# Layer 0's position bias: one more fold by DMA before the last product, one quarter of the sums on VectorE, and the tables on ScalarE

## The chip, the cores and the metric

The kernel runs on one core of a Trainium2 chip. The core has a matrix engine (TensorE, PE in the profile), VectorE (DVE), ScalarE (ACT), GpSimd (POOL) and a queue engine for transfers (SyncE, SP). Sixteen DMA engines move data for all of them. The metric is the device time of one execution in microseconds, lower is better; three runs of the kernel before gave 3259.31, 3259.72 and 3261.21, median 3259.72.

## The reference, cut to what matters

Four layers follow one another on an image batch. The change is in layer 0, a deformable attention on 2 images of 512 channels and 32 x 32 pixels, with 8 groups per image and 64 keys per group. Each key has a position that is computed from the data. For every one of the 1024 queries and every one of the 64 keys of a group, a small three-layer network turns the two coordinate differences into one number, the bias that is added to the attention score:

```python
pos = grid_q[:, :, None, :] - grid_kv[:, None, :, :]
bias = jnp.sign(pos) * jnp.log1p(jnp.abs(pos))
bias = jax.nn.relu(bias @ cpb_w1 + cpb_b1)      # 2 -> 128
bias = jax.nn.relu(bias @ cpb_w2 + cpb_b2)      # 128 -> 128
bias = (bias @ cpb_w3 + cpb_b3).reshape(b, GROUPS, H * W, Hd * Wd)
sim = jnp.einsum('bhid,bhjd->bhij', qh, kh) + bias
attn = jax.nn.softmax(sim, axis=-1)
out = jnp.einsum('bhij,bhjd->bhid', attn, vh)
```

That is 16 groups x 64 keys x 1024 queries through a network of width 128. All is in fp32.

## The kernel before, in words

**Tiling.** The loop over `quads` in `layer0` runs over 16 groups `u`, 8 steps `o` and two halves `half`: 256 quads of four keys each. A quad takes two calls. `first_hidden` makes the first hidden layer of four keys, 128 hidden units by 1024 queries for each key, with one VectorE instruction a key (L680): it adds a row table `x` and a column table `y`, broadcast against each other, and clips at zero. `second_hidden` multiplies these by the 128 x 128 weight (L704). A matmul makes 32 outputs of one key, and four keys stand side by side in the four strips of 32 rows of one PSUM tile, so a quad leaves four PSUM tiles, one for each quarter `q` of the 128 hidden units, each of 128 rows (4 keys x 32 units) by 1024 queries. Three such PSUM tiles exist (`c_ps_h`).

**The last layer.** The weights are sorted and scaled beforehand (`sorted_weights`), so that the last layer is a sum with signs. All quarters but the first hold units whose weights have the same sign in the same row, so quarters can be added without multiplying. ScalarE evicts each quarter with bias and ReLU (L709), multiplies the first by a sign (L711), GpSimd issues a DMA that adds the first quarter into the second (L716, 512 KB, accumulating), GpSimd adds the third into the fourth (L720), and one quad later `join` adds the second into the fourth (L723). The sum `z` has 32 rows a key. After a second half, `join` folds two quads: an accumulating DMA adds odd rows to even rows in the first half's sum (L725), another one even rows to odd rows in the second half's (L726), and SP copies the latter's odd rows into the former (L727). Then one tile holds eight keys with 16 rows each, and `last_product` sums the rows with a small matrix of signs on PE (L742): for every four quads one group of four matmuls, written to PSUM as scores. It is issued one such group of quads later, by the list `held`. `attend` adds query-key products, takes the softmax and multiplies by the values.

**The tables.** For two steps `o` at a time, SP loads `got`, the signed logarithms of the coordinate differences, from DRAM (L620). GpSimd makes `x` of it (L622, into SBUF); VectorE makes `y` (L665, into a PSUM bank) at the beginning of each first half. Two buffers exist for each of `got` and `x`.

**Order of the work.** The order on PE, ScalarE, VectorE and GpSimd is that of the program text. In each pass of the loop stand `first_hidden` of the next quad, `second_hidden` of this quad, perhaps a product, and then one step of the side work: `attend` and the output projection (`after`), or the positions, queries, keys and values of the next groups (`front`). So on ScalarE the order in a pass is: what `first_hidden` of the next quad puts there, the evictions of this quad, the step. On VectorE: the additions of the next quad, the step. Four buffers of h1 hold two quads.

**Buffers of the quarters.** Tags h20, h21, h22 and h23 have 2, 3, 2 and 6 buffers of 128 x 1024; the fourth holds `z` until its product or its copy is done.

The lines that the text below uses are L620, L622 and L665 (`table`), L680 (`first_hidden`), L704 to L727 (`second_hidden` and `join`), L742 (`last_product`), L366 (`share`'s and `projection`'s addition from PSUM) and L792 (the softmax's exponential).

Of the kernel before, what the change touches and what calls it, by code (L numbers as in the profile page):

```python
# [18 lines left out]
P = 128  # L19
# [16 lines left out]
    ("index", 1), ("row", 1), ("sixes", 16),  # L36
# [12 lines left out]
N_FOLDED, N_SINGLE = 56, 60  # L49
# [7 lines left out]
class Net:  # L57
# [40 lines left out]
    def layer0(self):  # L98
# [3 lines left out]
        with ExitStack() as ctx:  # L102
            keep = self.pool(ctx, "l0")
            self.l0qkv = keep.tile([P, 3, CT, P], F32, tag="qkv", name="qkv")
# [8 lines left out]
            self.l0w2 = keep.tile([P, P], F32, tag="w2", name="w2")  # L113
# [17 lines left out]
            self.hid2 = self.pool(ctx, "c_hid2", 1)  # L131
# [14 lines left out]
            with self.tc.manual_schedule(engines=engines):  # L146
# [23 lines left out]
                pairs[0]["xT"] = self.fone.tile([P, NB, P], F32, tag="xnT", name="xnT00")  # L170
# [15 lines left out]
                held, self.join, self.first_z = [], None, None  # L186
                batch = []
                for i, (u, o, half) in enumerate(quads):
# [9 lines left out]
                    z = self.second_hidden(u, o, half, h1, i + 1 == len(quads))  # L198
                    if half == 0:
                        batch.append((o % 2, z))  # L200
                    elif o % 2 == 1:
                        held.append((u, o, batch))
                        batch = []
                        if len(held) == 2:
                            v, last, zs = held.pop(0)
                            self.last_product(v, last, zs, sims, ps_s)
                            if last == 7:
                                if v == 8:
                                    self.advance(after, lambda: False)
                                    att = [  # L210
                                        apool.tile([P, N], F32, tag=f"att{t}", name=f"att{v}_{t}") for t in range(CT)
                                    ]
                                self.advance(front, lambda: "v" in pairs[v // 2])
                                after.append(self.attend(v, pairs[v // 2], sims.pop(v), att, ps))
                                if v % 8 == 7:
                                    after.append(self.projection(ps, att, ow, v // 8))
# [5 lines left out]
                (_, _, (ready, first)), = held  # L222
                self.last_product(u, o, [ready], sims, ps_s)
                self.single_product(u, o, 0, first[1], sims)
# [34 lines left out]
    def sorted_weights(self, keep):  # L259
# [7 lines left out]
        self.places = keep.tile([P, P + N_FOLDED + N_SINGLE], F32, tag="places", name="places")  # L267
        nc.scalar.dma_start(self.places, self.io["places"])
        before = keep.tile([P, P], F32, tag="before", name="before")
# [3 lines left out]
        names = ("pos", "six", "rest", "late", "gap", "neg", "first", "second", "rank", "mag", "sign")  # L273
# [8 lines left out]
        many = keep.tile([P, 16], F32, tag="many", name="sort_many")  # L282
        vec.tensor_tensor(many, self.colr("sixes", 16), total.to_broadcast([P, 16]), ALU.is_le)
        vec.tensor_reduce(c["six"], many, AX.X, ALU.add)
        vec.tensor_scalar(c["late"], c["six"], 6.0, None, ALU.mult)
        vec.tensor_scalar(c["rest"], c["six"], -6.0, 96.0, ALU.mult, ALU.add)
# [14 lines left out]
        pool.tensor_scalar(c["sign"], self.col("row"), c["six"], 2.0, ALU.is_lt, ALU.mult)  # L301
# [159 lines left out]
    def first_conv(self, qp, prod, conv, ps):  # L461
# [4 lines left out]
        for k in range(both, len(TAPS)):  # L466
            i = (k - both) % 8
            if i == 0:
                diag.append(self.hid2.tile([P, 8, P], F32, tag="h23", bufs=6, name=f"diag{k}"))
# [198 lines left out]
    def first_hidden(self, u, o, half, pairs, tables):  # L668

        if half == 0:  # L670
            tables["xy"] = self.table(u, o, pairs, tables)
# [1287 lines left out]
def _layout(i):  # L1959
# [10 lines left out]
    def over(v):  # L1970
        return np.broadcast_to(v.reshape(1, -1), (P, v.size))
# [59 lines left out]
```

## Time and profile before

| what | value |
|---|---|
| runs, us | 3259.31, 3259.72, 3261.21; median 3259.72 |
| the profiled execution, its own time | 3260.07 us |
| its span, first to last instruction | 3258.3 us |
| granted TensorE clock | 1.000 |
| L704, matmuls of layer 0's second hidden layer | 16384 records, 1784.0 us busy |
| L680, VectorE additions | 1028, 1210 ns each |
| L709, ScalarE evictions | 1024, 1110 ns each |
| L742, last product, 100 to 1900 us | 488 records, 64.3 us busy |
| L716, L725, L726: DMA issues on POOL | 255, 127, 127; issue to landing 5.4 us (512 KB), 5.0 us (256 KB) |
| L727, SP's copies | 127 of 256 KB; 4.0 us |
| L620, loads of the logarithms | 63 of 512 KB; 5.6 us |

In the profile a matmul in fp32 appears as two records, so a quad has 64. The busy time of an instruction is from its start to its end; on POOL an instruction can be recorded as started while the one before it still runs. "Idle before" with a releaser names the engine and line that ended the last wait. Layer 0 takes the first 1925 us or so of the span; the three other layers and layer 0's perceptron follow.

### The profile page before, as it was taken

To read this page: it belongs to the slowest core of one execution; us is meant where nothing else is said; L and a number is where in the kernel's file an instruction comes from. 1 tells how busy PE (TensorE), PEld (TensorE's weight loads), DVE (VectorE), ACT (ScalarE), POOL (GpSimd) and SP (SyncE) were. 2 spreads that over 40 slices of the span, in tenths; PEclk is the share of its full clock that TensorE was granted. 3 is DMA by queue.
4 is the path that set the end of the run, shared out by engine and by line. 5 is a ranking of instruction groups with operands and counts; after the bars stand their busy time and mean duration, and the time that the engine had idled before them with its cause. 6 is when DMAs were issued, how large, how long until landed. Compare 5 with 4: busy or idle time off the path is not lost.

```text
span 3258.3 us, 59109 instructions
## 1 busy us (share of the span) xinstructions
PE 3243.6 (100%) x24496; PEld 1210.7 (37%) x24496; DVE 2388.4 (73%) x2742; ACT 1949.1 (60%) x2013; POOL 2348.2 (72%) x1557
## 2 busy tenths in 40 slices
PE   9999999999999999999999999999999999999999
PEld 4333333333333333332333334444555533455333
DVE  7877878878877778878877765475555689855897
ACT  7787887887886687887887752111121466213662
POOL 7998998999998698999999972442323458634575
PEclk9999999999999999999999999999999999999999
DMA  6676776667766476667676662111000100000001
GB/s 171 144 152 136 152 148 143 146 146 146 149 145 127 104 153 139 142 143 146 149 145 145 145 158 78 39 39 39 1 1 1 40 1 2 14 1 14 1 1 53
DMA packets 96571, 309.35 MB, mean 95 GB/s; under 512 B 14688, under 2 KB 16864, under 8 KB 93216
## 3 DMA queue, kind: packets, MB, share of 16 engines
q0 software_dynamic: 57040, 200.31, 32.5%
q1 hardware_dynamic: 38240, 103.05, 9.7%
q8 instruction: 197, 3.23, 0.4%
q10 hardware_dynamic: 1008, 2.06, 0.2%
q14 instruction: 86, 0.70, 0.1%
HBM read 67.33 MB, written 4.46 MB: 22 GB/s over the span
## 4 chain that ended last, share of the span: by engine, by line
PE 81%; POOL 11%; DVE 5%; issue 2%; ACT 0%; DMA 0%; DVEq 0%; POOLq 0%; ACTq 0%; SPq 0%
PE hp L704 41%; PE s L1569 5%; PE o L1598 5%; POOL h L723 5%; POOL h L720 4%; PE qk30P L1344 1%; PE qk20P L1344 1%; PE m_7P L899 1%; PE m_6P L899 1%; PE m_4P L899 1%; PE m_2P L899 1%; PE m_0P L899 1%; PE qk31P L1344 1%; PE qk21P L1344 1%; PE m_5P L899 1%
## 5 line engine op out<-in xcount | busy, mean ns | idle before, releaser
L704 PE MATMUL hp<-h,w2s 128*32 128x512 f32 x16384 | 1784.0, 592 | 0.5 <-DVE h L680 0.2
L680 DVE CUSTOM_DVE_ANT_1 h<-tx,bank 128x1024 f32<-128x1024 f32 (+1 forms) x1028 | 1180.3, 1210 | 301.9 <-PE hp L704 240.3
L709 ACT ACTIVATE h<-hp,magb 128x1024 f32<-128x1024 f32 x1024 | 1133.1, 1110 | 378.8 <-PE hp L704 368.2
L704 PEld LDWEIGHTS hp<-h,w2s 128*32 128x32 f32 x16384 | 530.6, 110 | 1212.5 <-issue 1184.6
L720 POOL TENSOR_TENSOR h<-h,h 128x1024 f32<-128x1024 f32 x255 | 819.1, 3212 | 1.6 <-ACT h L709 1.6
L723 POOL TENSOR_TENSOR h<-h,h 128x1024 f32<-128x1024 f32 x254 | 751.3, 2958 | 0.0
L716 POOL DMA_DIRECT2D h<-h x255 | 303.0, 1188 | 192.3 <-ACT h L709 179.6
L1573 ACT ACTIVATE e<-s 128x1024 f32<-128x1024 f32 x256 | 262.0, 1025 | 181.1 <-PE s L1569 176.5
L711 ACT ACTIVATE h<-h,flip 128x1024 f32<-128x1024 f32 x256 | 294.3, 1150 | 8.4
L1598 PE MATMUL o<-e,v 64*64 64x512 f32 x2048 | 265.2, 589 | 2.2 <-DVE q L1637 2.2
L1569 PE MATMUL s<-q,k 64*64 64x512 f32 x2048 | 265.9, 591 | 0.0
L1580 POOL TENSOR_TENSOR some<-some,e 128x1024 f32<-128x1024 f32 x64 | 168.2, 2629 | 26.2 <-ACT e L1573 23.3
L1578 POOL TENSOR_TENSOR some<-e,e 128x1024 f32<-128x1024 f32 x32 | 76.1, 2379 | 141.3 <-DVE sum L1587 102.3
L726 POOL DMA_DIRECT2D h<-h x127 | 175.4, 1381 | 1.0 <-issue 1.0
L725 POOL DMA_DIRECT2D h<-h x127 | 149.0, 1173 | 0.0
L1585 DVE TENSOR_TENSOR sum<-sum,e 128x1024 f32<-128x1024 f32 x64 | 124.6, 1947 | 28.8 <-ACT e L1573 26.1
L869 POOL TENSOR_TENSOR mlp_w<-mlp_w 128x512 f32<-128x512 f32 x16 | 22.3, 1391 | 165.0 <-DMA mlp_w<-in_mlp_w 111.2
L1598 PEld LDWEIGHTS o<-e,v 64*64 64x64 f32 x2048 | 77.8, 133 | 145.1 <-issue 134.9
L1569 PEld LDWEIGHTS s<-q,k 64*64 64x64 f32 x2048 | 76.5, 133 | 133.2 <-issue 117.5
L960 ACT ACTIVATE mh<-mh,cols 128x512 f32<-128x512 f32 x64 | 46.1, 721 | 124.3 <-DVE mh L978 65.4
L1583 DVE TENSOR_TENSOR sum<-e,e 128x1024 f32<-128x1024 f32 x32 | 81.5, 2547 | 31.7 <-ACT e L1573 31.6
L1332 POOL TENSOR_TENSOR sq<-q 128x512 f32<-128x512 f32 x32 | 33.2, 1041 | 96.1 <-DVE q L1351 54.2
(572 smaller groups left out, 3365.2 us busy)
## 6 DMA issues: line engine op xcount, KB each, us to landing
h<-h POOLq DMA_DIRECT2D x255, 512.0 KB, 5.4
h<-h POOLq DMA_DIRECT2D x254, 256.0 KB, 5.0
h<-h SPq DMA_DIRECT2D x127, 256.0 KB, 4.0
lb<-logs SPq DMA_DIRECT2D x63, 512.0 KB, 5.6
mlp_w<-in_mlp_w SPq DMA_DIRECT2D x16, 1024.0 KB, 4.9
x<-in_x SPq DMA_DIRECT2D x8, 512.0 KB, 7.5
qkw<-in_l_qk SPq DMA_DIRECT2D x2, 2048.0 KB, 7.7
out<-x SPq DMA_DIRECT2D x15, 256.0 KB, 2.0
```

The costliest lines, as they stand in the source:

```text
L680: self.nc.vector._custom_dve(TENSOR_ADD_SAT, out=h1[r][:, k, cut, :], in0=x[:, 4 * half + 2 * r + k, :].unsqueeze(1).to_broadcast([P, H // ...
L704: nc.tensor.matmul(hp[rows, cut], lhsT=self.l0w2[:, 32 * q : 32 * q + 32], rhs=h1[k][:, cut], start=True, stop=True)
L709: nc.scalar.activation(y, hp, AF.Relu, bias=self.magb[:, q, 0:1])
L711: nc.scalar.activation(y, y, AF.Copy, scale=self.flip)
L716: nc.gpsimd.dma_start(y, ys[0], accum_op=ALU.add)
L720: (nc.vector if final else nc.gpsimd).tensor_tensor(y, y, ys[2], ALU.add)
L723: (nc.vector if final else nc.gpsimd).tensor_tensor(z, z, other, ALU.add)
L726: nc.gpsimd.dma_start(z[1::2, :], z[0::2, :], accum_op=ALU.add)
L899: self.nc.tensor.matmul(acc[p], lhsT=w[:, a, k, p * P : (p + 1) * P], rhs=right(r, k), start=k == 0, stop=k == 1)
L1569: nc.tensor.matmul(s[halves[c], par, :], lhsT=ks[p][rows, at : at + DH], rhs=qs[p][rows, cut], start=True, stop=True)
L1573: nc.scalar.activation(e, s, AF.Exp, scale=DH**-0.5)
L1598: nc.tensor.matmul(o[halves[par], r, :], lhsT=v[n // 2][rows, n % 2, at : at + DH], rhs=e[rows, par, :], start=(n == 0), stop=(n == NB - 1),)
```

## The change

- Sums are folded once more. Two tiles of folded sums (16 rows a key, eight keys) become one tile of sixteen keys with 8 rows a key. New function `refold`, called from `second_hidden` two quads after a second half: two accumulating DMAs of 32 rows on GpSimd, then one or two copies of 32 rows by SP. The copy that stood in `join` stays only in the last eight quads. The last product, `twice_product`, then comes once in eight quads, four quads after the group's last; `folded_product` (16 rows a key) and `single_product` (32 rows) serve the end.
- In a second half with even `o` (`fused`, two of eight quads) VectorE evicts the third quarter: `max` with minus its bias, plus the second quarter. The bias that this leaves out is added to the first quarter by ScalarE's multiplication by the sign. The DMA that adds the first quarter goes to the third quarter's tile, after VectorE, and `join` adds that tile to the fourth. GpSimd's addition L720 is left out there.
- `x` and `y` are made by ScalarE: `y` at the beginning of a first half, `x` at the beginning of the second half after its load was issued.
- The sorting of the weights goes by groups of twelve instead of six. Buffers of h23 rise from 6 to 9. To make room, the sampling tiles share one tile with the convolution's products, and some small tiles of the beginning share one h23 buffer.

```diff
@@ layer0
-                pairs[0]["xT"] = self.fone.tile([P, NB, P], F32, tag="xnT", name="xnT00")
+                self.sampling(pairs[0], 0)
...
-                    z = self.second_hidden(u, o, half, h1, i + 1 == len(quads))
+                    z = self.second_hidden(i, u, o, half, h1, firsts, len(quads) - 8, i + 1 == len(quads))
                     if half == 0:
-                        batch.append((o % 2, z))
-                    elif o % 2 == 1:
-                        held.append((u, o, batch))
-                        batch = []
-                        if len(held) == 2:
-                            v, last, zs = held.pop(0)
-                            self.last_product(v, last, zs, sims, ps_s)
-                            if last == 7:
...
+                        firsts.append(z)
+                    elif o % 4 == 1 and ready_set:
+                        v, e, zs = ready_set
+                        self.twice_product(v, e, zs, sims, ps_s)
+                        ready_set = None
+                        if e == 1:
...
+                    elif o % 4 == 3:
+                        if i + 1 < len(quads):
+                            ready_set = u, o // 4, firsts[:2]
+                            firsts = []
+                        else:
+                            self.folded_product(u, o - 2, firsts[:2], sims, ps_s)
@@ table
-            nc.gpsimd.tensor_scalar(x, got[:, :, :, 0, :], self.col("cpb_w1", 0), self.col("cpb_b1"), ALU.mult, ALU.add)
...
-        nc.vector.tensor_scalar(y, tables["logs"][:, jj, :, 1, :], self.col("cpb_w1", 1), None, ALU.mult)
+        nc.scalar.activation(y, tables["logs"][:, jj, :, 1, :], AF.Copy, scale=self.col("cpb_w1", 1))
@@ first_hidden
         if half == 0:
             tables["xy"] = self.table(u, o, pairs, tables)
+        elif "next" in tables:
+            got, x = tables["next"]
+            self.nc.scalar.activation(
+                x, got[:, :, :, 0, :], AF.Identity, scale=self.col("cpb_w1", 0), bias=self.col("cpb_b1")
+            )
@@ second_hidden
+        fused = half == 1 and o % 2 == 0
...
-            y = self.hid2.tile([P, N], F32, tag=f"h2{q}", bufs=(2, 3, 2, 6)[q], name=f"h2_{u}_{o}{half}{q}")
+            y = self.hid2.tile([P, N], F32, tag=f"h2{q}", bufs=(2, 3, 2, 9)[q], name=f"h2_{u}_{o}{half}{q}")
             ys.append(y)
+            if q == 3 and self.refolds and self.refolds[0][0] <= i:
+                self.refold(*self.refolds.pop(0)[1:])
+            if fused and q == 2:
+                vec.scalar_tensor_tensor(y, hp, self.under, ys[1], ALU.max, ALU.add)
+                pool.dma_start(y, ys[0], accum_op=ALU.add)
+                continue
             nc.scalar.activation(y, hp, AF.Relu, bias=self.magb[:, q, 0:1])
-            if q == 0:
+            if q == 0 and fused:
+                nc.scalar.activation(y, y, AF.Identity, scale=self.flip, bias=self.magb[:, 2, 0:1])
+            elif q == 0:
                 nc.scalar.activation(y, y, AF.Copy, scale=self.flip)
             elif q == 1:
                 if final:
-                    nc.vector.tensor_tensor(y, y, ys[0], ALU.add)
-                else:
-                    nc.gpsimd.dma_start(y, ys[0], accum_op=ALU.add)
+                    vec.tensor_tensor(y, y, ys[0], ALU.add)
+                elif not fused:
+                    pool.dma_start(y, ys[0], accum_op=ALU.add)
                 if self.join:
                     self.join(final)
-            elif q == 3:
-                (nc.vector if final else nc.gpsimd).tensor_tensor(y, y, ys[2], ALU.add)
+            elif q == 3 and not fused:
+                (vec if final else pool).tensor_tensor(y, y, ys[2], ALU.add)
...
+        def join(final, z=ys[3], other=ys[2 if fused else 1], first=self.first_z, fold=half == 1 and not final):
+            (vec if final else pool).tensor_tensor(z, z, other, ALU.add)
             if fold:
-                nc.gpsimd.dma_start(first[0::2, :], first[1::2, :], accum_op=ALU.add)
-                nc.gpsimd.dma_start(z[1::2, :], z[0::2, :], accum_op=ALU.add)
-                nc.sync.dma_start(first[1::2, :], z[1::2, :])
+                pool.dma_start(first[0::2, :], first[1::2, :], accum_op=ALU.add)
+                pool.dma_start(z[1::2, :], z[0::2, :], accum_op=ALU.add)
+                if last:
+                    nc.sync.dma_start(first[1::2, :], z[1::2, :])
+
+        if half == 1 and not last:
+            self.refolds.append((i + 2, firsts[o % 4 % 2], self.first_z, ys[3], o % 4 // 2))
...
+    def refold(self, to, even, odd, second):
+        nc = self.nc
+        add, dma = ALU.add, nc.gpsimd.dma_start
+        if second:
+            dma(even[2::4, :], even[0::4, :], accum_op=add)
+            dma(odd[3::4, :], odd[1::4, :], accum_op=add)
+            nc.sync.dma_start(to[2::4, :], even[2::4, :])
+            nc.sync.dma_start(to[3::4, :], odd[3::4, :])
+        else:
+            dma(to[0::4, :], to[2::4, :], accum_op=add)
+            dma(odd[1::4, :], odd[3::4, :], accum_op=add)
+            nc.sync.dma_start(to[1::4, :], odd[1::4, :])
```

## The prediction

> **What bounds the kernel now.** I read the page's busy line and chain first, to see which engine never rests and for how much of the span:
>
> ```profile
> span 3258.3 us, 59109 instructions
> ...
> PE 3243.6 (100%) x24496; PEld 1210.7 (37%) x24496; DVE 2388.4 (73%) x2742; ACT 1949.1 (60%) x2013; POOL 2348.2 (72%) x1557
> ...
> PE 81%; POOL 11%; DVE 5%; issue 2%; ACT 0%; DMA 0%; DVEq 0%; POOLq 0%; ACTq 0%; SPq 0%
> ```
>
> TensorE is busy throughout. The change lies in layer 0's bias, which fills about 1925 of the 3258 us. The windows view of its middle (columns: PE, PEld, DVE, ACT, POOL busy, clock, DMA share, GB/s) shows that PE hardly pauses and that POOL is next:
>
> ```profile
> 400.00:800.00 400.00, 400.00 (x3768) 121.67 (x3764) 319.01 (x355) 320.96 (x315) 366.91 (x244) 1.00 0.69 146
> ```
>
> The chain of waits over 600 to 700 us gives the unit of the sums below. A quad (four keys, one call of second_hidden) is 64 matmul records and takes 6.87 us; a product group (last_product) is 8 records and 0.86 us:
>
> ```profile
> 599.72 6.87 PE hp L704 x64
> 606.58 0.86 PE sim L742 x8
> 607.44 13.73 PE hp L704 x128
> ```
>
> Then POOL's groups, 100 to 1900 us. The reader is to see that POOL idles only 173.5 us in 1800, nearly all for ScalarE's second eviction:
>
> ```profile
> L720 POOL TENSOR_TENSOR h<-h,h 128x1024 f32<-128x1024 f32 x243 | 782.2, 3219 | 0.0
> L723 POOL TENSOR_TENSOR h<-h,h 128x1024 f32<-128x1024 f32 x243 | 720.0, 2963 | 0.0
> L716 POOL DMA_DIRECT2D h<-h x242 | 288.8, 1193 | 173.5 <-ACT h L709 160.8 <-issue 10.9 <-DMA h<-h 1.6
> L726 POOL DMA_DIRECT2D h<-h x121 | 167.1, 1381 | 1.0 <-issue 1.0
> L622 POOL TENSOR_SCALAR tx<-lb,cols 128x512 f32<-128x512 f32 x60 | 93.7, 1562 | 0.0
> ```
>
> POOL's spans overlap, so prices come from one end to the next end in its timeline:
>
> ```profile
> 612.94 0.88 POOL L716 DMA_DIRECT2D h<-h  x1 [0.79 <-ACT h L709]
> 613.55 2.70 POOL L723 TENSOR_TENSOR h<-h,h 128x1024 f32<-128x1024 f32 x1
> 615.88 1.17 POOL L725 DMA_DIRECT2D h<-h  x1
> 616.54 1.39 POOL L726 DMA_DIRECT2D h<-h  x1
> 617.12 3.23 POOL L720 TENSOR_TENSOR h<-h,h 128x1024 f32<-128x1024 f32 x1
> ```
>
> Ends 613.82, 616.25, 617.05, 617.93, 620.35: an add costs 2.42, a DMA issue 0.80 and 0.88 (0.83 to 0.88 elsewhere), though it only issues. L622 costs 0.74 so. An add that follows an idle POOL takes 2.70.
>
> Last, ScalarE and VectorE at a softmax step (quad 55 starts at 424.02):
>
> ```profile
> 424.30 1.11 ACT L709 ACTIVATE h<-hp,magb 128x1024 f32<-128x1024 f32 x1 [0.57 <-PE hp L704]
> 425.43 1.28 ACT L792 ACT_TABLE_LOAD   x1
> 426.73 0.72 ACT L792 ACTIVATE t<-t,cols 128x512 f32<-128x512 f32 x1
> ...
> 424.32 4.61 DVE L680 CUSTOM_DVE_ANT_1 h<-tx,bank 128x1024 f32<-128x1024 f32 x4 [1.82 <-PE hp L704]
> ```
>
> The four VectorE additions of the next quad start 0.30 us into a quad and end at 4.91, almost 2 us before PE needs them, whatever ScalarE is doing.
>
> **What the Trainium skill says.** "Perfetto Trace Analysis", section GPSIMD Engine Instruction: POOL's reported spans do not add up and spacing should be used; the trace agrees (spans of 3.2 us, 2.4 apart). "DMA: Bandwidth & Descriptors", section Anatomy of one DMA: a POOL DMA takes about 2.0 us plus bytes/436 GB/s, an estimate of 3.2 us for 512 KB; the page here has 5.4 from issue to landing for these accumulating ones, which is used. "ScalarE: Activation LUTs", section What ACT_TABLE_LOAD costs: 186 ns plus 0.833 ns an element, 93 for each per-partition operand, about 93 of overlap. The trace agrees for 1024 elements from SBUF with one such operand (1.13 against L711's 1.15) and for the load (1.28).
>
> **Part 1, the second fold: fewer products.** Before, 63 full product groups and a half; after, 31 twice_product groups, one folded and the half. 31 x 0.86 = 26.7 us leave PE's queue, and PE is the bound: -26.7. In the stretch 100 to 1900, without the 28.5 us of the output projection (L358), 242.2 quads take 1771.5 us, 29.26 for four; without half a product group, 28.83.
>
> **Part 2, tables on ScalarE.** y (L665, 0.48 on VectorE) was written ahead. On ScalarE it is queued behind the fourth eviction of the quad before last and that iteration's step. Price by the skill's formula for 256 elements and one operand: 0.49, 0.39 after overlap. Eviction ends 1.39 us into the quad, y at 1.78, VectorE's four end at 1.85 + 4.61 = 6.46, PE needs them at 6.87: hidden by 0.3. Where ScalarE has a step in between it is not: behind the softmax above (end 3.43), 3.43 + 0.39 + 0.07 + 4.61 + 0.10 = 8.60 against 6.86 (the product group that used to stand there is gone): 1.74 late. I did this for every first half from ScalarE's timeline: 7 softmax steps with a load 12.2, 7 without 2.2, and six of gelu, logarithm, weights and q copies 4.3. Sum +18.7, serial, as the next quad's additions wait for PE again. If y took 0.30 it would be about 16; at 0.80, the some 70 quiet first halves without a product group ahead of them stand at the edge. x (L622, now two per-partition operands, 0.80 by the formula) comes before a first eviction, with three PSUM buffers giving about 1.5 us of room: 0. But it waits for the lb load, which SP issues behind the refold copies; by the landings below it lands about 1.5 us before ScalarE asks if POOL is punctual, so late by what POOL lags beyond that. Bounds 0 and +10; I take 0.
>
> **Part 3, VectorE evicts the third quarter** in 64 of 256 quads. No row has it; the nearest is L366, PSUM plus SBUF, 128x1024, 1283 ns (a ScalarE eviction is 1110). It starts behind the four additions at 6.47, ends at 7.75; PE wants that PSUM buffer at about 8.6: hidden. What follows on VectorE starts late: step work above 1.2 us in such a quad delays the next additions. VectorE's timeline has two or three such steps in 32 quads, 0.2 to 0.5 over: +5 (0 to +8).
>
> **Part 4, POOL.** Per four quads one add (-2.42) and one x table (-0.74) go and four refold issues come (+3.4): busy time hardly changes, 26.8 to 27.1. What is new is a wait. In the fused quad the DMA that adds ys[0] into ys[2] is issued after VectorE, and the join, one quad later and only two refold issues and one DMA issue behind it, waits for its landing. Everything on POOL stands behind that join. From the end of that issue round to the next: landing 4.1 (from the end of the issue, L716 landings average 5.4, 4.2, 3.9 and 4.0 for the four quads of a group; I take the last three, as the first meets the lb load); join from idle 2.70; two folds 1.69; add 2.42; issue 0.83; join 2.42; two refolds 1.69; add 2.42; issue 0.83; join 2.42; two folds 1.69; add 2.42; join that needs this add's end 2.75; issue 0.81. Sum 29.2. A loop of 29.2 against PE's 28.83 + (18.7 + 5)/61 = 29.22: equal, and equal to the 29.26 of before.
>
> **Part 5, refold to product.** From that issue's end: refolds land behind it at about 5.2 (an estimate from 4.1 and L726), SP's two copies take 4.0 (page), product at 9.3. PE comes to it three quads after the fused quad's start, at 20.6 + 1.0 of other matmuls; the issue ends at 9.4 when POOL is punctual: 2.9 us of room for POOL to lag.
>
> Prologue and tail have the same steps but for details: 0. Sum: -26.7 + 18.7 + 5 = -3; two coupled queues of equal pace with 2.9 us between them cost something where either is late, +5 by judgement (0 to +15). Together +2 on 3258.3. The profiled run took 3260.07, 0.35 above the median 3259.72; 1.8 us lie outside its span. Forecast 3262.
>
> **Rivals.** (A, forecast) The saving is given back to ScalarE's late tables and POOL's loop: 3252 to 3268, centre 3262. For: both sums meet 29.26. Chance 0.37.
> (B, slower) POOL's loop decides. Place: the join behind the fused DMA. Point: each 0.1 us of landing above 4.1 costs 0.1 x 61 = 6 us. DMA bytes grow about 9% for four quads (4096 to 4480 KB at the page's sizes) and the class beside the lb load lands in 5.4. At 4.5: +24 on the forecast, 3286; at 5.4 about 3340. Refold lag would stall PE here, at sim. Against: nothing but its own followers is in flight with it. Chance 0.35.
> (C, faster) ScalarE's steps fall elsewhere or are short, and POOL, with 2.9 us of room, is never late: the 26.7 less the 12.2 of the softmax, about 3245; less nothing, 3233. For: POOL idles 2.8 us per four quads now. Against: the softmax rows. Chance 0.28.
> That the products do not halve I exclude: the loops fix their number.
>
> **Numbers.** A measurement of this kernel can tell about 0.2%, 6.5 us. A lies within that for 0.29 and above for 0.08; B is slower, C faster: faster 0.28, same 0.29, slower 0.43. Range 3243 to 3290: A whole, most of C, B to a landing of about 4.55. A's own is 3252 to 3268.
>
> **What would show it.** sim products half as many, PE's idle before hp released by DVE additions that wait for ACT bank (part 2: near 19 us, over 1.5 at each softmax with a load); POOL idle at the join, released by a DMA, of about 1.5 us each of 64 times, little at L716's successor; no idle before the sim products. I am wrong if PE idles before sim (B), if first halves start on time (C), or if y takes well over 0.6 us.

## The result, and the profile after

The changed kernel takes 3290.72 us (median of four runs, 3285.34 to 3294.48) against 3259.75 before: a ratio of 1.0093, 95% interval 1.0080 to 1.0106. It is 31 us slower. The forecast was 3262, with a range of 3243 to 3290. The profiled run took 3294.48 us, 3.8 above the median.

The page of the changed kernel, the same three lines as before:

```profile
span 3292.8 us, 59295 instructions
...
PE 3255.7 (99%) x24248; PEld 1274.1 (39%) x24248; DVE 2418.7 (73%) x2680; ACT 1969.8 (60%) x2138; POOL 2357.4 (72%) x1678
...
PE 70%; POOL 14%; DVE 9%; issue 4%; ACT 1%; DMA 1%; DVEq 0%; POOLq 0%; SPq 0%; ACTq 0%
```

TensorE has 248 matmul records fewer, yet it is "busy" 12 us longer and at 99%. In an undisturbed quad, such as quad 36 of the changed kernel, the records start in fours within 0.02 us. In quad 37, where the operands came late, the first six start one by one, 0.4 to 0.7 us apart, each about as long as before (592 to 617 ns); the quad takes 10.0 us, and TensorE counts as busy for all of them. So the busy share hides the loss, and the chain shows it: PE's share fell from 81 to 70%, VectorE's and POOL's rose. I therefore measured TensorE in another way: for each record, the time by which it moves the end of TensorE's work, summed over the 64 records of a quad (6.87 us when nothing disturbs it), over the product records, and over what follows the last hp matmul. "hp" is the name of the PSUM tiles that the second hidden layer's matmuls write.

| kernel, profiled run | hp over 6.87, quads 8 to 249 | products | behind the last hp | span |
|---|---|---|---|---|
| before | 9.9 | 56.3 | 1333.9 | 3258.3 |
| after | 56.9 | 32.9 | 1340.1 | 3292.8 |

The last products come behind the last hp matmul, so 3.1 us of the products are in the column behind it too, in both kernels.

So the products gave 23.4 us, the second layer's matmuls took 47.0 more, and what follows layer 0's quads takes 6.2 us more. Side work's small matmuls (L413) account for 3.4 more; together 33 of the 34.5 us of difference.

Where the 47 us wait is seen in the groups, 100 to 1900 us (busy, mean ns, idle time before and its releasers), first two of the kernel before, then those of the changed kernel:

```profile
L704 PE MATMUL hp<-h,w2s 128*32 128x512 f32 x15500 | 1687.2, 592 | 0.4 <-DVE h L680 0.2
L680 DVE CUSTOM_DVE_ANT_1 h<-tx,bank 128x1024 f32<-128x1024 f32 x971 | 1119.0, 1215 | 287.9 <-PE hp L704 231.0 <-ACT bank L570 25.3 <-ACT at L411 23.9
```

```profile
L721 PE MATMUL hp<-h,w2s 128*32 128x512 f32 x15257 | 1689.1, 593 | 15.3 <-DVE h L729 12.3 <-ACT h L732 1.3
L795 PE MATMUL sim<-h,signed 128*32 128x512 f32 x240 | 34.4, 593 | 0.8 <-DMA h<-h 0.8
...
L695 DVE CUSTOM_DVE_ANT_1 h<-tx,bank 128x1024 f32<-128x1024 f32 x954 | 1099.6, 1214 | 335.3 <-ACT bank L675 294.5 <-PE hp L721 22.7 <-ACT bank L575 9.2
...
L513 DVE TENSOR_SCALAR xn<-x,bn1s,cols 128x1024 f32<-128x1024 f32 x6 | 32.9, 5490 | 0.0
...
L675 ACT ACTIVATE bank<-lb,cols 128x256 f32<-128x256 f32 x119 | 56.2, 472 | 27.1 <-DVE bank L841 18.2 <-DVE prod L391 7.2 <-DVE h L695 1.7
...
L750 POOL TENSOR_TENSOR h<-h,h 128x1024 f32<-128x1024 f32 x238 | 651.1, 2736 | 19.8 <-DMA h<-h 14.5
```

Three things are to be seen. VectorE's additions (L695; L680 before) used to wait for TensorE, 231.0 of 287.9 us, that is, they were early; now they wait for ScalarE's y (L675), 294.5 of 335.3. POOL's join (L750) waits only 14.5 us for landings: POOL's loop through the fused DMA, case B, isn't what costs the 31 us here. And the six instructions named xn take 5490 ns on average: four of them 7.7 to 7.9 us, the two others 0.8 and 1.1.

One of those four, in VectorE's and then POOL's timeline of the changed kernel (start, duration, engine, line):

```profile
526.12 7.74 DVE L513 TENSOR_SCALAR xn<-x,bn1s,cols 128x1024 f32<-128x1024 f32 x1
533.78 2.34 DVE L695 CUSTOM_DVE_ANT_1 h<-tx,bank 128x1024 f32<-128x1024 f32 x2
...
526.03 3.17 POOL L750 TENSOR_TENSOR h<-h,h 128x1024 f32<-128x1024 f32 x1
528.35 1.65 POOL L774 DMA_DIRECT2D h<-h  x1
528.92 1.94 POOL L775 DMA_DIRECT2D h<-h  x1
529.49 3.81 POOL L745 TENSOR_TENSOR h<-h,h 128x1024 f32<-128x1024 f32 x1
```

The same instruction in the kernel before, and POOL beside it:

```profile
516.64 1.89 DVE L509 TENSOR_SCALAR xn<-x,bn1s,cols 128x1024 f32<-128x1024 f32 x1
...
514.75 3.23 POOL L720 TENSOR_TENSOR h<-h,h 128x1024 f32<-128x1024 f32 x1
517.38 1.43 POOL L716 DMA_DIRECT2D h<-h  x1
518.06 3.19 POOL L723 TENSOR_TENSOR h<-h,h 128x1024 f32<-128x1024 f32 x1
```

In the changed kernel it is recorded as started 0.09 us behind a POOL addition, and ends 0.56 us after the end of the second one, with the two new refold issues between them (L774, L775). In the kernel before it ends 0.56 us after the end of the first addition, though the second one follows at once. The Trainium skill, "SBUF — State Buffer", section Who interferes with whom, says that VectorE and GpSimd share a pair of ports, and that of two instructions which need it the one that starts later is blocked for the whole of the other. The case agrees for one addition, and adds something that a single pair doesn't cover: here VectorE got nothing between two additions either. Over all traces of this case, for xn and for the small product log times pos (128x64, of the key positions) where they began during an addition, what stood on POOL between that one and the next went with the outcome. With the two refold issues between them (14 times), or with the second addition recorded as started before the first had ended (20 times), VectorE ended 0.09 us (log) or 0.56 us (xn) after the second. With one issue of the first quarter's DMA between them, as in the kernel before, it ended by as much after the first, all 63 times. Why the one lets VectorE in and the other doesn't is not shown. The chain of the changed kernel shows what follows:

```profile
528.56 5.19 PE hp L721 x48
533.75 0.03 issue
533.78 4.60 DVE h L695 x4
...
541.09 0.49 ACT bank L675
541.57 0.02 issue
541.60 2.24 DVE h L695 x2
```

VectorE's additions start at 533.78 instead of about 528; the softmax step behind them is late on VectorE; y (L675) waits for that step, which writes the same PSUM bank; and the next additions wait for y, until 541.60. Such waits of y for the softmax's bank are the 18.2 us in L675's line above; where xn is on ScalarE (e2 below) they come to 0.4 us.

### The profile page after: what moved, and what is told of

Its sections match the earlier page's. It is cut to its first block, busy times and chain, and to the rows that moved or that the text cites. A ratio compares the mean times of both kernels' runs of the same rounds, so it can differ in the third digit from the quotient of the medians.

```text
span 3292.8 us, 59295 instructions
## 1 busy us (share of the span) xinstructions
PE 3255.7 (99%) x24248; PEld 1274.1 (39%) x24248; DVE 2418.7 (73%) x2680; ACT 1969.8 (60%) x2138; POOL 2357.4 (72%) x1678
## 4 chain that ended last, share of the span: by engine, by line
PE 70%; POOL 14%; DVE 9%; issue 4%; ACT 1%; DMA 1%; DVEq 0%; POOLq 0%; SPq 0%; ACTq 0%
PE hp L721 32%; PE s L1622 5%; PE o L1651 5%; POOL h L750 4%; DVE h L695 3%; POOL h L745 3%; POOL h L741 2%; PE qk30P L1397 1%; PE qk20P L1397 1%; PE m_7P L952 1%; PE m_5P L952 1%; PE m_4P L952 1%; PE m_2P L952 1%; PE m_0P L952 1%; PE qk31P L1397 1%
## 5 line engine op out<-in xcount | busy, mean ns | idle before, releaser
L721 PE MATMUL hp<-h,w2s 128*32 128x512 f32 x16384 | 1813.3, 593 | 15.4 <-DVE h L729 12.3
L695 DVE CUSTOM_DVE_ANT_1 h<-tx,bank 128x1024 f32<-128x1024 f32 (+1 forms) x1028 | 1180.4, 1210 | 358.7 <-ACT bank L675 315.4
L732 ACT ACTIVATE h<-hp,magb 128x1024 f32<-128x1024 f32 x960 | 1056.9, 1108 | 356.0 <-PE hp L721 354.7
L721 PEld LDWEIGHTS hp<-h,w2s 128*32 128x32 f32 x16384 | 598.8, 110 | 1192.2 <-issue 1007.2
L750 POOL TENSOR_TENSOR h<-h,h 128x1024 f32<-128x1024 f32 x254 | 694.1, 2733 | 20.6 <-DMA h<-h 14.9
L745 POOL TENSOR_TENSOR h<-h,h 128x1024 f32<-128x1024 f32 x191 | 635.6, 3327 | 1.6 <-ACT h L732 1.6
L741 POOL DMA_DIRECT2D h<-h x191 | 230.6, 1207 | 156.3 <-ACT h L732 155.9
L736 ACT ACTIVATE h<-h,flip 128x1024 f32<-128x1024 f32 x192 | 220.7, 1150 | 6.3
L753 POOL DMA_DIRECT2D h<-h x127 | 168.7, 1328 | 2.1 <-issue 2.1
L752 POOL DMA_DIRECT2D h<-h x127 | 157.4, 1239 | 0.0
L922 POOL TENSOR_TENSOR mlp_w<-mlp_w 128x512 f32<-128x512 f32 x16 | 21.2, 1324 | 169.2 <-DMA mlp_w<-in_mlp_w 127.3
L1385 POOL TENSOR_TENSOR sq<-q 128x512 f32<-128x512 f32 x32 | 33.2, 1039 | 96.2 <-DVE q L1404 54.3
```

Of the source, the lines that this page charges most:

```text
L695: self.nc.vector._custom_dve(TENSOR_ADD_SAT, out=h1[r][:, k, cut, :], in0=x[:, 4 * half + 2 * r + k, :].unsqueeze(1).to_broadcast([P, H // ...
L721: nc.tensor.matmul(hp[rows, cut], lhsT=self.l0w2[:, 32 * q : 32 * q + 32], rhs=h1[k][:, cut], start=True, stop=True)
L732: nc.scalar.activation(y, hp, AF.Relu, bias=self.magb[:, q, 0:1])
L736: nc.scalar.activation(y, y, AF.Copy, scale=self.flip)
L741: pool.dma_start(y, ys[0], accum_op=ALU.add)
L745: (vec if final else pool).tensor_tensor(y, y, ys[2], ALU.add)
```

## The experiments

Each kernel is the one named, with the edit shown. Medians and ratios are to the kernel before, run beside it. The table at the end of this section has every run.

**1. Is it y on ScalarE, xn, or POOL?** y back on VectorE alone; xn on ScalarE alone; both; and the other way round, the kernel before with nothing but y on ScalarE.

```diff
# e1 (and e3), in table
-        nc.scalar.activation(y, tables["logs"][:, jj, :, 1, :], AF.Copy, scale=self.col("cpb_w1", 1))
+        nc.vector.tensor_scalar(y, tables["logs"][:, jj, :, 1, :], self.col("cpb_w1", 1), None, ALU.mult)
# e2 (and e3), in normed, for all but the first tiles
-        (ahead or nc.vector).tensor_scalar(
-            xn, self.xs[b][t], self.s1[:, t : t + 1], self.col("bn1_b", t), ALU.mult, ALU.add
-        )
...
+            nc.scalar.activation(xn, self.xs[b][t], AF.Identity, scale=self.s1[:, t : t + 1], bias=self.col("bn1_b", t))
# e4: the kernel before, with the first edit reversed
```

> The changed kernel with y alone back on VectorE (L675 of the changed kernel becomes the VectorE multiplication of before). Theory L (late tables: y behind ScalarE's evictions and softmax steps starts VectorE's additions late, and the lateness is carried into the fused quads): the seven softmax steps and what they carry go, 12 to 25 us less than the changed kernel's 3290.7, so 3266 to 3279; PE's idle before hp halves. Theory P (POOL's loop through the fused DMA's landing): within 4 us of 3290.7. Theory X (the VectorE normalisation xn of 7.7 us, which waits for POOL): its five or six places stay at 7.7 us, so no more than what L gains.

> The changed kernel with the normalisation xn (L513, once in 32 quads) on ScalarE instead of VectorE. Theory X: five places where a quad is 4.2 us late lose most of it, 15 to 21 us less, 3270 to 3276. Theory L: the lateness at these places comes from y, which waits for VectorE's softmax operations, and stays: within 4 us of 3290.7. Theory P: within 4 us.

> Both: y on VectorE and xn on ScalarE in the changed kernel. Theories L and X together: 3290.7 less 27 to 46, so 3245 to 3264; at 3240 or below PE alone would be the bound (3259.7 less the 26.7 of the products is 3233). Theory P: above 3280.

> The kernel before with y alone on ScalarE, one part of the change by itself. Theory L: by the sum of the prediction with the product groups still in place (a softmax step with a load is 0.9 late there instead of 1.7) 8 to 12 us more than 3259.7, so 3268 to 3272. Theories P and X: no change, 3258 to 3262.

Measured: 3267.08, 3277.02, 3266.40 and 3290.22 us. y explains 23.6 us, xn 13.7 when taken alone and nothing once y is back. Moving y alone in the kernel before costs 30.6 us, as much as the whole change. In e1 the time didn't go where it had come from, though. The hp matmuls fell by 40.6 us and the products rose by 25.2. The profiled run of e1 is the slowest of its twelve (3274.78 us), but that of e3, 0.5 us above its median, shows the same: 43.6 less and 20.6 more. The products of e1, then of e3:

```profile
L795 PE MATMUL sim<-h,signed 128*32 128x512 f32 x240 | 48.2, 600 | 13.6 <-DMA h<-h 12.1 <-POOL h L745 1.3
...
L798 PE MATMUL sim<-h,signed 128*32 128x512 f32 x248 | 47.9, 595 | 10.3 <-DMA h<-h 9.7 <-POOL h L748 0.5
```

Half as many products now take about as long (58.1 and 53.5 us) as all of them before (56.3): they wait for the refolds. The saving of the second fold was lost twice over, and the late y only hid the second loss. So three questions followed: why y is so dear, what the tail of 6 us is, and what the product waits for.

**2. Is y dear because of its place?** y is issued a quad and more earlier, behind the third eviction of the first half before (e7 in the changed kernel, e8 in the kernel before with y on ScalarE). Then, in e8's kernel, one small VectorE operation, log times pos, is given to GpSimd (r10).

```diff
# e7, e8: y leaves table; in second_hidden of a first half
             nc.scalar.activation(y, hp, AF.Relu, bias=self.magb[:, q, 0:1])
+            if q == 2 and self.ahead:
+                self.next_y(*self.ahead)
# r10 = e8 and
-            nc.vector.tensor_tensor(log, log, pos, ALU.mult)
+            nc.gpsimd.tensor_tensor(log, log, pos, ALU.mult)
```

> The changed kernel with one edit: ScalarE writes y right behind the third eviction of the first half before, ahead of the fourth eviction and of the step, and so 8 us earlier. Theory L (the 24 us that y on ScalarE costs are y standing late in ScalarE's queue): 3268 us (3264 to 3272), as with y on VectorE. Rival X (VectorE's xn and its like blocked behind POOL's additions are the cause, and y on VectorE helped only because it moved them): 3278 to 3291. Rival S (ScalarE has not the time for y wherever it stands): 3285 to 3291.

> The kernel before with y on ScalarE, which alone took 3290.2 us, and with y at the early place. Theory L: nearly all of the 30 us go, 3261 us (3259 to 3265). Rival X: the 13 us at the softmax quads whose VectorE logarithm operation took 5.6 us remain, 3272 to 3278. Rival S: 3285 to 3291.

> The kernel before with y early on ScalarE, which took 3278.0 us, and with the one operation log times pos (L441 of the kernel before, seven times, 128x64) on GpSimd instead of VectorE. Theory X (its loss is the five softmax quads in which this operation, started on VectorE just as POOL began two additions in a row, took 5.6 to 5.9 us and held up the next quad's additions by 2.9): 3264 us (3260 to 3267), five stalls of 2.9 gone. Rival S (the loss is ScalarE's time for y, and the long operation only a mark of it): 3275 to 3279.

Measured: e7 3264.72, e8 3277.97, r10 3260.67 us. In the changed kernel the place of y is the whole of its cost, and e7 is even as good as y on VectorE. In the kernel before, neither theory held alone: 12 us went with the early place and 18 stayed, where the rival had put them. In the kernel before with y alone on ScalarE (e4), VectorE's and POOL's timelines show it:

```profile
420.74 5.62 DVE L441 TENSOR_TENSOR log<-log,pos 128x64 f32<-128x64 f32 x1
426.28 1.21 DVE L680 CUSTOM_DVE_ANT_1 h<-tx,bank 128x1024 f32<-128x1024 f32 x1
...
420.43 3.50 POOL L723 TENSOR_TENSOR h<-h,h 128x1024 f32<-128x1024 f32 x1
422.77 3.49 POOL L720 TENSOR_TENSOR h<-h,h 128x1024 f32<-128x1024 f32 x1
```

An operation on 64 elements a partition, 0.84 us in the kernel before, takes 5.62 us because it arrives just behind the start of POOL's two additions; quad 55's own additions then start at 426.28. In e4 this meets all six xn (5.65 to 5.88 us) and five of the logs (5.60 to 5.64 us); in e8 the xn are quick again (1.78 to 1.83, but one) and five logs still take 5.86 to 5.89. With the log on POOL, about 1.4 us there, the kernel with y on ScalarE is at par with the kernel before (ratio 0.9995 to 1.0012). So ScalarE's time for y costs nothing that can be seen in the kernel before: what costs is y's late place, and that VectorE's work shifts against POOL's.

**3. The tail.** e3 with layer 0's pools laid out in the old order. The changed kernel allocates the second layer's buffers right behind the constants, so that the first normalised tiles of the following feed-forward part fall on buffers which the last products still read.

```diff
# e5 = e3 and
             keep = self.pool(ctx, "l0")
+            self.fpool = self.pool(ctx, "f", 2)
+            self.fone = self.pool(ctx, "f1", 1)
+            self.lpool = self.pool(ctx, "c_log", 2)
+            self.tab = self.pool(ctx, "c_tab", 2)
+            self.hid = self.pool(ctx, "c_hid", 4)
             self.hid2 = self.pool(ctx, "c_hid2", 1)
```

> The changed kernel with y back on VectorE and xn on ScalarE, as in the run before it that took 3266.4 us, and with the five SBUF pools of layer 0 laid out ahead of the pool of second layer tiles, as in the kernel before. Theory T (layer 0's last sums now lie where the feed-forward part's first normalised tiles go, so these wait for the last product; worth the 5 to 6 us by which everything behind layer 0's quads got longer): 3261 us (3259 to 3263), and the stretch behind the last hp matmul is 1334 us again instead of 1339. Rival (the tail is longer for another cause, such as the last group's own products): 3265 to 3268 and 1339.

Measured: 3264.09 us, and 1333.2 behind the last hp instead of 1339.1. The tail is settled by that stretch; the median fell by 2.3 only, and the runs of e5 lie between 3258.1 and 3267.6 us where those of the kernel before lie between 3259.2 and 3261.8. The wait in VectorE's and TensorE's timelines, e3:

```profile
1935.46 0.17 DVE L95 TENSOR_SCALAR bn2s<-cols 128x4 f32<-128x4 f32 x1 [5.79 <-PE sim L809]
...
1949.33 0.53 PE L868 MATMUL bank<-pt,v 64*64 64x256 f32 x2 [4.28 <-DVE pt L857]
```

The small scaling bn2s waits 5.79 us for the last product (the releaser in brackets), the normalisations behind it on VectorE then fall into the last softmax, and TensorE waits 4.28 us for that. In e5 and in the kernel before the matmul of pt and v has no such wait.

**4. The wait for the refolds.** The product is issued one quad later (e6). On this: the third quarter given back to ScalarE and POOL everywhere (r9), xn back on VectorE (r11); and the changed kernel with early y, old pool order and late product together (r12).

```diff
# e6 = e5 and
-                    elif o % 4 == 1 and ready_set:
+                    if half == 0 and o % 4 == 2 and ready_set:
...
-                    elif o % 4 == 3:
+                    elif half == 1 and o % 4 == 3:
# r9 = e6 and
-        fused = half == 1 and o % 2 == 0
+        fused = False
```

> The same, and the product of two folded groups stands one quad (6.9 us) later in TensorE's order. Theory R (what is left of the loss in the middle is TensorE waiting before the product for refold and copies, about 10 to 15 us, because POOL lags by more than the 2.9 us of room): those waits go, 3248 us (3244 to 3254), faster than the kernel before. Rival P (POOL's loop sets the pace, TensorE only happens to meet it at the product): the wait shows before hp instead, through late buffers, and the time stays within 3 us of the run without this edit, about 3258 to 3264.

> The run with the product one quad later (3256.4 us), and ScalarE evicts and POOL adds every third quarter, as in the kernel before; the second fold and its refolds stay. Theory P4 (POOL cannot carry the refolds besides all the additions; by the distances between ends it would need 8 additions of 2.42, 8 fold and refold issues of 0.85 and 4 issues of 0.83 us, 29.5 us for four quads, against 28.83 of TensorE): 3280 us (3272 to 3295). Rival (POOL has the room, and VectorE's part of the third quarter saves nothing): 3251 to 3261.

> The run with the product one quad later (3256.4 us), with xn back on VectorE as in the changed kernel. Its hp matmuls take 18 us more than those of the kernel before, 12 of them at the quads 39, 71, 103, 135 and 199. Theory N (these are ScalarE's time for xn and what follows it): 3248 us (3244 to 3252). Rival X (on VectorE xn falls behind a run of POOL additions and takes 7.7 us, as in the changed kernel): 3258 to 3268.

> The changed kernel with the three mends together: y early on ScalarE, the pools of layer 0 in the old order, and the product one quad later. Theory R and T (the three losses stand side by side and add): from 3264.7 us with y early alone, 6 for the tail and 8 to 12 for the waits before the product go, 3249 us (3245 to 3254). Rival (POOL's loop takes the waits back before hp): 3256 to 3262.

Measured: 3256.40, 3285.19, 3256.36 and 3262.77 us. In e6 the products fall to 32.2 us, with no idle time before them:

```profile
L798 PE MATMUL sim<-h,signed 128*32 128x512 f32 x248 | 32.8, 592 | 0.0
```

So theory R is right about the wait; but the hp matmuls rise from 13.8 to 28.5 and the tail by 2.9, so more than half is taken back, as rival P had it. r9 comes out near the 3280 of theory P4, and POOL's idle time falls from 154 us in e6 to 40, so POOL is nearly full. But the path of the loss is another one than that theory's: of 31.7 us more in the hp matmuls, 26.2 lie in quads 84, 116, 180 and 212, behind a VectorE operation of 128x2 on the key positions (L420). It began beside a POOL addition with two refold issues and another addition behind it, and took 5.2 to 6.5 us; in e6 five of its seven took 0.15 and the others about 1. So r9 shows what the fused quarter is worth, but not that POOL can't carry the refolds. r11 is a plain miss: xn isn't what is left. r12 is a miss too; the mends don't add.

**5. What holds these versions at 3256?** In e6 POOL waits at the join for the fused DMA, as case B of the prediction had it, 63 times and 1.2 us each (line, releaser, total us, times, longest):

```profile
POOL h L753 <- DMA h<-h: 76.9, 63, 4.7
```

And the chain of e6, at 300 to 306 us, runs through VectorE:

```profile
301.30 1.19 DVE h L732
302.50 0.64 DVE t L840
...
305.30 0.36 DVE h L698
```

L732 is the eviction of the third quarter; the softmax step comes behind it, and only then the additions (L698). r13 puts POOL's own addition ahead of the join in the quad behind a fused one; r14 does so in r12's kernel. r15 is r13, and r16 is e6, with the third quarter left to ScalarE and POOL in one fused quad of each eight, the one ahead of that softmax step.

```diff
# r13, r14
+        late_join = half == 0 and o % 2 == 1
-                if self.join:
+                if self.join and not late_join:
                     self.join(final)
             elif q == 3 and not fused:
                 (vec if final else pool).tensor_tensor(y, y, ys[2], ALU.add)
+                if late_join:
+                    self.join(final)
# r15, r16
-        fused = half == 1 and o % 2 == 0
+        fused = half == 1 and o % 2 == 0 and i % 32 != 5
```

> The run with the product one quad later (3256.4 us, the kernel of e6_product_later), and in the quad behind a fused one POOL does that quad's own addition (L748) before the join, so that the join meets the landing of the fused DMA behind work instead of idle. Theory B (what is left is POOL's loop through that landing: POOL idles at the join 63 times, 77 us in all, and the quads go at 29.12 us for four against TensorE's 28.83): the idle at the join goes to under 15 us, the quads go at 28.9, 3243 us (3238 to 3250). Rival (POOL only idles there because others are late; ScalarE's waits for free second layer buffers set the pace): 3253 to 3259, and POOL idles elsewhere.

> The same with the change's own tables on ScalarE, y early (the three mends, 3262.8 us, and the late join). Theory B: its join idles too (86 us, 73 times), so it gains as much, 3250 us (3244 to 3256). Rival (there the shared bank of y holds VectorE and ScalarE up): 3259 to 3264.

> The run with the join late (3256.9 us), and in one fused quad of eight pairs, the one before the softmax (seven or eight in all, quads 37, 69, 101 and so on), the third quarter is left to ScalarE and POOL as in the kernel before. Theory V (what keeps this run from its 3243 is VectorE: in the quads 39, 71, 103, 135 and 199 and their next the hp matmuls take 2.3 us too long, and the chain there runs through VectorE's eviction of 1.2 us and the softmax step behind it): five to seven stalls of about 2 us go, 3246 us (3243 to 3251). Rival P (POOL has not the time for these additions either): 3255 to 3260.

> The same without the late join (against 3256.4 us). Theory V: the same stalls go, 3247 us (3244 to 3252). Rival P: POOL, which idled 77 us at the join and still set the pace, gets 2.4 us more to do in such a quad and loses them: 3256 to 3264.

Measured: 3256.94, 3263.65, 3251.39 and 3260.11 us. In r13 POOL's idle time only moved:

```profile
POOL h L749 <- ACT h L736: 82.0, 57, 1.9
```

It now waits for ScalarE's fourth eviction, and the time stands still: theory B fell for r13 and r14 alike. Part of r13's gain is hidden by its end: its hp matmuls take 1.3 us less than e6's, its tail 3.3 more. r15 and r16 tell the two limits apart. With the join late (r15), taking VectorE's eviction away ahead of the softmax gains 5.5 us, and the 1.3 us in quads 39, 71, 135 and 199 are gone (0.48 is left of it in quad 103). With the join where it was (r16) the same edit loses 3.7 us. In r16's profiled run, the fastest of its thirteen, those stalls are gone as well, but others came, in quads 18, 87 and 242 above all, and POOL idles 85.4 us at the join instead of 76.9; that it is the additions given back to POOL which cost the time is the rival's account, and likely, but that run doesn't show the loss. VectorE and POOL hold these versions together, and neither mend shows alone. r15, which keeps the second fold, x on ScalarE and VectorE's eviction in seven of eight fused quads, with y on VectorE and xn on ScalarE, falls short of its 3246, but it beats both kernels: ratio to the kernel before 0.9975, 0.9964 to 0.9985.

The tail of r15 (1339.3 us against 1333.9) is its own doing. TensorE waits 5.35 us for a landing before one of the last products, against 1.16 in the kernel before. With the join behind POOL's own addition, the last fold is issued only 0.4 us before the last hp matmul ends (4.8 in the kernel before), and its landing and SP's copy come after that. With the join late everywhere but in the last quads this might be saved; no run tried it.

The products of the table include the last ones behind the last hp, which the last column counts too: 3.1 to 3.6 us of them in e1 to e5, e7, e8 and r10, and 4.5 to 8.1 in e6, r9 and r11 to r16. Without these, the products take 53.2 us in the kernel before and 26.6 in e6.

| run | what it is | median us | ratio, 95% interval | hp over 6.87 | products | behind last hp |
|---|---|---|---|---|---|---|
| e1 | after, y on VectorE | 3267.08 | 1.0021, 1.0012 to 1.0030 | 16.3 | 58.1 | 1339.8 |
| e2 | after, xn on ScalarE | 3277.02 | 1.0052, 1.0035 to 1.0069 | 39.5 | 32.9 | 1340.4 |
| e3 | both | 3266.40 | 1.0020, 1.0009 to 1.0031 | 13.3 | 53.5 | 1339.1 |
| e4 | before, y on ScalarE | 3290.22 | 1.0094, 1.0077 to 1.0111 | 37.6 | 56.3 | 1333.5 |
| e5 | e3, pools as before | 3264.09 | 1.0011, 1.0003 to 1.0020 | 13.8 | 55.3 | 1333.2 |
| e6 | e5, product later | 3256.40 | 0.9990, 0.9984 to 0.9997 | 28.5 | 32.2 | 1336.1 |
| e7 | after, y early | 3264.72 | 1.0012, 1.0005 to 1.0019 | 18.9 | 44.7 | 1339.8 |
| e8 | e4, y early | 3277.97 | 1.0054, 1.0040 to 1.0068 | 27.3 | 56.8 | 1333.7 |
| r9 | e6, no quarter on VectorE | 3285.19 | 1.0074, 1.0059 to 1.0089 | 60.2 | 31.7 | 1335.8 |
| r10 | e8, log on POOL | 3260.67 | 1.0003, 0.9995 to 1.0012 | 10.4 | 56.3 | 1334.8 |
| r11 | e6, xn on VectorE | 3256.36 | 0.9988, 0.9981 to 0.9994 | 30.7 | 31.2 | 1336.1 |
| r12 | e7, pools, product later | 3262.77 | 1.0008, 0.9999 to 1.0016 | 35.2 | 33.2 | 1338.0 |
| r13 | e6, join later | 3256.94 | 0.9990, 0.9984 to 0.9997 | 27.2 | 34.7 | 1339.4 |
| r14 | r12, join later | 3263.65 | 1.0012, 1.0006 to 1.0019 | 34.2 | 34.7 | 1338.5 |
| r15 | r13, eight quads less on VectorE | 3251.39 | 0.9975, 0.9964 to 0.9985 | 21.2 | 34.7 | 1339.3 |
| r16 | e6, the same | 3260.11 | 1.0001, 0.9993 to 1.0009 | 30.3 | 31.1 | 1334.2 |

## Why the prediction was wrong, point by point

- **Part 1, the products (-26.7).** Right: -23.4 in the profile of after, and -26.6 within the quads of e6, where nothing waits at the product.
- **Part 2, y on ScalarE (+18.7). This is the term that failed.** The mechanism was right (VectorE's additions wait for ScalarE's y) and so were the durations: 0.472 us for y against 0.49, 0.808 for x against 0.80, and 1.0 to 1.6 us lost in the quad of each softmax against 1.74. But the sum followed y in ScalarE's queue alone and let VectorE's other work stand where it stood. In the hp matmuls y cost 26.2 us (e2 against e3), and 17.4 more came from xn (after against e2), which, shifted, fell behind a run of POOL's additions: 43.6 us where the sum had 18.7. Part 2 named neither that nor y's own waits for VectorE's work on the same PSUM bank. These are the softmax, late behind xn, and the convolution's multiplications (L391): in e2 y waits 1.4 us for the latter five times, and the quad behind each is 1.6 us late. In e7, with y early and no such wait, the same quads are still 1.5 us late, so how much that wait costs is open. The cost in the median, 23.6 us in the changed kernel, is net of the wait for the refolds that it hid. x was taken as 0; ScalarE waited 0.4 us before it in all, but no run has it alone.
- **Part 3, VectorE's eviction (+5).** The duration was right (1276 ns against 1283). The cost behind a softmax step is real, about 6 us of hp time in r15 against r13, but it can't be seen in the changed kernel.
- **Part 4, POOL's loop.** "Busy time hardly changes" was right (2357 us on POOL against 2348). The fused quarter is worth its place (r9 takes 28.8 us more than e6), though most of r9's loss doesn't run through POOL's loop. The loop didn't decide in the changed kernel (14.5 us of landing waits), and the 1.5 us at each of 64 joins that case B described came up as 1.2 us at 63 joins in e6, when the other losses were gone.
- **Part 5, 2.9 us of room between refold and product.** Wrong as soon as y is on time: the products take 25.2 us more in e1 and 20.6 in e3 than in the changed kernel. The durations were no longer than taken (in e3 refolds land in 4.5 us and a copy takes 3.0, against 5.2 and 4.0), so it is the time at which POOL issues the refolds that was off; the traces were not followed further. In the changed kernel the stalls of y gave the refolds the time they lacked, and "no idle before the sim products" came true for the wrong reason.
- **Prologue and tail (0).** Wrong by 6.2 us. The diff moved one pool, and with it the addresses that the next part of the network reuses.
- **The sum.** Replaced term by term it reads -23.4 + 47.0 + 3.4 + 6.2 = 33 in the profiled run, where the prediction had -26.7 + 18.7 + 5 + 5 + 0 = 2. "Given back to ScalarE's late tables" was the right case with less than half of its size; it was given more chance than case B by a little, and its range of 3252 to 3268 didn't hold the time, which lies even above the whole range to 3290. Case B's 3286 is nearer to the time, but by chance: the wait that it rests on is 14.5 us in all.

Still open: 11 us of r15's hp matmuls beyond those of the kernel before have no cause shown. That VectorE's block ends only with the second addition was read from timelines. r10 tested what it costs for the log; for xn, e2 took it away but moved the work to another engine as well.

## What to carry to other kernels

When an operation is moved to an engine with time to spare, ask what its new lateness does to the consumer's other work, above all to VectorE instructions that may now start beside GpSimd's long ones. Where several engines go at nearly the same pace, removing one wait shows the next: here the late y, the wait for the refolds, POOL's join and VectorE's eviction hid one another, and the last two mends gained nothing one by one (r13, r16) and 5 us together (r15 against e6). And when a pool of buffers is moved, look at what the following stage lays over it.

## What the runs showed of the hardware that was not expected

- A VectorE product of 128x64 took 4.3 to 6.4 us, a 128x1024 scaling 5.5 to 7.9 us and, in r9, an operation of 128x2 5.2 to 6.5 us, when they began beside two GpSimd additions in a row, even with two refold issues between these; in the kernel before the first two took 0.76 to 1.38 and 1.82 to 1.89 us, but for one scaling of 5.53. With one issue of the first quarter's DMA between the two additions, VectorE got in after the first, all 63 times. On GpSimd itself the small product was recorded with 0.6 to 1.5 us.
- A busy share of 99% on TensorE hid most of 47 us of waiting: the idle time before the hp matmuls grew by 15 us only (0.4 to 15.3), and the rest lay in matmuls of about the same length that no longer ran side by side.
